# Depthwise 3x3 convolutions: from nine VectorE passes to nine TensorE products with diagonal weights

## The chip, the cores and the metric

The kernel runs on one core of a Trainium2 chip. The metric is the device time of that core in microseconds (us). Engines are named as in the profile: PE (TensorE; PEld its weight loads), DVE (VectorE), ACT (ScalarE), POOL (GpSimd), SP (SyncE, which issues most DMAs).

## The reference, cut to what matters

Eight images of 64 channels and 64x64 pixels, fp32, pass through four blocks. Three places compute a depthwise 3x3 convolution (each channel with its own nine weights, zero padding):

```python
# block 0: attention over all 4096 pixels, then
out = conv3x3_depthwise(att, w2); out = relu(bn2(out))
x = bn3(einsum('bchw,oc->bohw', out, w3)) + x
# block 1: two rounds of window attention and an MLP; block 2: dynamic filters and a 1x9 convolution
# block 3: a selective scan of four directions, sixteen states each
xi, z = split(einsum('bhwc,dc->bhwd', ln(x), in_proj_w) + in_proj_b)
xc = silu(conv3x3_depthwise(xi, conv_w) + conv_b)           # 128 channels
y = ln(sum of the four scans of xc) * silu(z);  x = einsum(y, outproj_w) + x
# block 3, last part: channels in four groups, group i max-pooled by 2**i
s_i = repeat(conv3x3_depthwise(maxpool(part_i, 2**i), mfr_w[i]) + mfr_b[i], 2**i)
out = gelu(einsum('bchw,oc->bohw', concat(s_0..s_3), aggr_w) + aggr_b) * n + x
```

## The kernel before, in words

Two images are worked on at once: their 2 x 64 channels are the 128 partitions, and the 4096 pixels are eight chunks of 512 columns (8 rows of 64). There are four such pairs. `front(p)` is everything of pair p up to the inputs of the scan (`layer0`, `layer1`, `layer2`, `scan_sources`), `scans(p)` is its selective scan, and `back(p)` is what follows.

`begin` runs `front(0)` by itself, with `alone` true. Then `scans(p)` goes through 64 units of 512 pixels with eight steps each, 512 steps a pair, two states a step. In a step, POOL multiplies B by du (L1788), ACT makes the exponentials `dad` (L1810), DVE runs the two recurrences (L1813), POOL and DVE multiply by C (L1824, L1827), and PE sums the states into `yd` (L1839), two or three steps later. Fetches of B and C are DMAs on SP's queue. For the last pair, and during the attention, DVE takes more of the products with C (`own`).

Beside the steps of `scans(p)` a generator hands out `back(p-1)` and `front(p+1)` piece by piece: each `yield` names a cost, and a step takes so many pieces that the costs grow evenly over the steps. For the last pair there is only `back(2)`, at twice the pace; `back(3)` comes with the last units and after them. The program's order is the generator's; a list scheduler then places every instruction by priority and its own estimate of when an engine is free, so an engine's queue may hold pieces ahead of older steps. Each engine works its queue in order.

The convolutions are in `_Direct.dwconv` (L1249): for a chunk, the first tap is a multiplication of the shifted, padded image by the channel's weight (L1257 or L1259) into a PSUM bank, and the other eight are multiply-adds on that bank (L1255), all on DVE.
- In `layer0` the result `cacc` goes through ACT (Relu, batch norm) to the product `pw` (L1348).
- In `scan_sources`, one image at a time, the result is `xacc`: all 128 channels, from the padded `XI`, with the bias in the first tap. ACT applies Silu (`xcv`, L1653), copies it transposed (`XT`), and sends it off by DMA; `z` (L1672) comes from a product of its own, `pz`.
- In `back`, the normalised image `F` is max-pooled three times. Each pooled image is convolved on DVE (`net.dwconv`, L436 and L438) and widened by ACT into `big` (L1909). Then each chunk is convolved (`sacc`), copied by ACT (`S`), and multiplied with its 1x1 weights (L1922); three more products (L1926) add the pooled groups, and Gelu follows (L1933).

PSUM's eight banks are divided: three for chunk results of the front (`f`), one for its accumulators, three for the scan (`da`), one for `yd`.

Of the kernel before, what the change touches and what calls it, by code (L numbers as in the profile page):

```python
# [9 lines left out]
F32 = mybir.dt.float32  # L10
AF = mybir.ActivationFunctionType
ALU = mybir.AluOpType
# [3 lines left out]
B, C, HH, WW = 8, 64, 64, 64  # L16
L = HH * WW
P = 128
CH = 512
# [3 lines left out]
TAPS = 9  # L23
# [1136 lines left out]
class _Direct:  # L1160
# [73 lines left out]
    def normed(self, wk, srcs, cen, avg, eps, out_view=None, bufs=None):  # L1234
# [11 lines left out]
        nc.scalar.activation(sd, sd, AF.Exp, scale=-0.5)  # L1246
        return pc, sd

    def dwconv(self, dst, pad, at, n, wt, bias, cost=0.5):  # L1249

        nc = self.nc
        for t in range(TAPS):
            src = pad[:, at + t // 3 : at + t // 3 + n, t % 3 : t % 3 + 64]
            if t:
                nc.vector.scalar_tensor_tensor(dst, src, wt[:, t : t + 1], dst, ALU.mult, ALU.add)  # L1255
            elif bias is None:
                nc.vector.tensor_scalar(dst, src, wt[:, 0:1], None, ALU.mult)  # L1257
            else:
                nc.vector.tensor_scalar(dst, src, wt[:, 0:1], bias, ALU.mult, ALU.add)  # L1259
            yield cost  # L1260


    def front(self, p):
# [5 lines left out]
    def layer0(self, p):  # L1269


        nc, tc, w, net, half = self.nc, self.tc, self.w, self.net, self.HALF
        X = self.flat("X")
        nc.sync.dma_start(X, self.net.x[2 * p : 2 * p + 2].rearrange("b c h w -> (b c) (h w)"))
        att = self.padded("att")
        VT = self.flat("VT").rearrange("p (t c) -> p t c", c=P)

        def at(rows, t):
            return X[rows, t * P : (t + 1) * P]

        with self.work("w0") as wk:
            for g in range(8):
                pv = self.bank("pval", (P, 4, P))
                nc.tensor.matmul(pv, lhsT=net.ones[0:1, :], rhs=net.b1row.rearrange("o a c -> o (a c)").unsqueeze(1).to_broadcast([1, 4, P]), start=True, stop=False)
                for j in range(4):
                    nc.tensor.matmul(pv[:, j, :], lhsT=at(slice(0, P), 4 * g + j), rhs=net.w1bd, start=False, stop=(j == 3))
                nc.scalar.activation(VT[:, 4 * g : 4 * g + 4, :], pv, AF.Relu)
                yield 3

            parts = wk.tile([P, 2, 32, NCH], F32, name="parts", tag="parts", bufs=1)  # L1290
            self.dense = 1
            for jc in range(NCH):
                po = self.total("po")

                def weigh(t, es):
                    for im in range(2):
                        nc.tensor.matmul(  # L1297
                            po[half[im]], lhsT=VT[:, t, half[im]], rhs=es[im], start=(t == 0), stop=(t == 31)
                        )

                last = None
                for t in range(32):
                    ss = [self.bank(f"s{im}") for im in range(2)]
                    for im in range(2):
# [12 lines left out]
                    last = (t, es)  # L1317
                    yield 3.6
                weigh(*last)
                nc.vector.tensor_copy(self.rows(att, jc), self.img(po))  # L1320

            self.dense = 0
            sums = net.sums[:, p]
            nc.vector.tensor_reduce(sums, parts, AX.X, ALU.add)
            rec = wk.tile([P, 2, 32], F32, name="rec", tag="rec", bufs=1)
            nc.vector.reciprocal(rec, sums)
            for g in range(8):
                pr = self.bank("prec")
                for j in range(4):
                    for im in range(2):  # L1330
                        nc.tensor.matmul(
                            pr[half[im], j * P : (j + 1) * P],
                            lhsT=rec[:, im, 4 * g + j : 4 * g + j + 1].to_broadcast([P, 64]),
                            rhs=w["ident"],
                            start=True,
                            stop=True,
                        )
                d = self.rows(att, g)
                nc.vector.tensor_tensor(d, d, self.img(pr), ALU.mult)
                yield 3  # L1340
        with self.work("w0b") as wk:
            for c in range(NCH):
                acc = self.bank("cacc", (P, 8, 64))
                yield from self.dwconv(acc, att, 8 * c, 8, w["dw2"], None, 0.52)
                cv = wk.tile([P, 8, 64], F32, name="cv", tag="cv")
                nc.scalar.activation(cv, acc, AF.Relu, scale=net.bn23[:, 0:1], bias=net.bn23[:, 1:2])
                pw = self.bank("pw")
                nc.tensor.matmul(pw, lhsT=w["w3bd"], rhs=cv, start=True, stop=True)  # L1348
                nc.scalar.activation(pw, pw, AF.Identity, scale=net.bn23[:, 2:3], bias=net.bn23[:, 3:4])
                x = X[:, c * CH : (c + 1) * CH]  # L1350
                nc.vector.tensor_tensor(x, x, pw, ALU.add)
                yield 2.25
        return X
# [271 lines left out]
    def scan_sources(self, p, X2):  # L1625
# [2 lines left out]
        x2 = self.memory("x2")  # L1628
        with tc.tile_pool(name="w3", bufs=2) as wk:
            H = self.flat("H3")  # L1630
            for c in range(NCH):
                cols = slice(c * CH, (c + 1) * CH)
                nc.sync.dma_start(x2[:, cols], X2[:, cols])
# [4 lines left out]
            for im in range(2):  # L1638
# [9 lines left out]
                XT = self.flat("XT").rearrange("p (w h) -> p h w", h=64)  # L1648
                for c in range(NCH):
                    acc = self.bank("xacc", (P, 8, 64))  # L1650
                    yield from self.dwconv(acc, pad, 8 * c, 8, w["cw"], w["cb"])
                    cv = wk.tile([P, 8, 64], F32, name="xcv", tag="xcv")
                    nc.scalar.activation(cv, acc, AF.Silu)  # L1653
                    last = nc.scalar.activation(XT[:, 8 * c : 8 * c + 8, :], cv, AF.Copy)
                    nc.scalar.dma_start(xc[:, c * CH : (c + 1) * CH], cv.rearrange("p a b -> p (a b)"))
                    yield 1.4
# [5 lines left out]
                for c in range(NCH):  # L1662
# [5 lines left out]
                        start=True,  # L1668
                        stop=True,
                    )  # L1670
                    z = wk.tile([P, CH], F32, name="z", tag="z")
                    last = nc.scalar.activation(z, pz, AF.Silu, bias=w["in_b"][:, 1:2])  # L1672
                    nc.scalar.dma_start(zs[:, c * CH : (c + 1) * CH], z)
                    yield 1.4
# [186 lines left out]
    def back(self, p):  # L1861
# [26 lines left out]
                yield 4.2  # L1888
        with tc.tile_pool(name="w5", bufs=1) as wk:
            prev, n, ups = F, 64, []  # L1890
            for i in range(1, 4):
                n //= 2
                at = (0, 1024, 1536)[i - 1]
# [4 lines left out]
                net.pad_border(pool, n + 2, nc.vector)  # L1898
                h2 = hf.rearrange("p (h two) w -> p h two w", two=2)
                nc.vector.tensor_tensor(pool[:, 1 : n + 1, 1 : n + 1], h2[:, :, 0, :], h2[:, :, 1, :], ALU.max)  # L1900
                if i == 1:
                    cv = big[:, 0:1024].rearrange("p (a b) -> p a b", b=n)
                else:
                    cv = wk.tile([P, n, n], F32, name=f"cv{i}", tag=f"cv{i}")
                net.dwconv(cv, pool, w["mw"][:, i, :], w["mb"][:, i : i + 1], n)
                k = 2**i
                at = (2048, 0, 1024)[i - 1]
                up = big[:, at : at + 64 * n].rearrange("p (a b) -> p a b", b=64)
                nc.scalar.activation(  # L1909
                    up.rearrange("p h (w k) -> p h w k", k=k), cv.unsqueeze(3).to_broadcast([P, n, n, k]), AF.Copy  # L1910
                )
                ups.append(up)
                prev = pool
                yield 7
            for c in range(NCH):
                cols = slice(c * CH, (c + 1) * CH)
                acc = self.bank("sacc", (P, 8, 64))
                yield from self.dwconv(acc, F, 8 * c, 8, w["mw"][:, 0, :], w["mb"][:, 0:1])
                S = wk.tile([P, 8, 64], F32, name="S", tag="S", bufs=2)
                nc.scalar.activation(S, acc, AF.Copy)  # L1920
                pa = self.bank("pa", (P, 8, 64))
                nc.tensor.matmul(pa, lhsT=w["agT"][:, 0, :], rhs=S, start=True, stop=False)  # L1922
                for i in range(1, 4):
                    k = 2**i
                    r = 8 // k
# [4 lines left out]
                        start=False,  # L1930
                        stop=(i == 3),
                    )
                last = nc.scalar.activation(pa, pa, AF.Gelu, bias=w["aggr_b"])  # L1933
                nc.vector.tensor_tensor(pa, pa, self.rows(F, c), ALU.mult)
                nc.vector.tensor_tensor(X[:, cols], X[:, cols], pa.rearrange("p a b -> p (a b)"), ALU.add)
                nc.sync.dma_start(out[:, cols], X[:, cols])
# [53 lines left out]
```

## Time and profile before

| | us |
|---|---|
| median of 3 runs (lowest, highest) | 12034.72 (12024.86, 12036.76) |
| the profiled execution | 12027.92 |
| its span, first to last instruction | 12026.1 |
| busy: PE, DVE, POOL, ACT | 9286.0, 8501.9, 7496.6, 7041.5 |
| mean granted PE clock | 0.856 |
| layer 0's convolution, `cacc`: alone; beside scans | 56; 132, 136, 136 |
| scan_sources from its first H to the last z, beside scans | 232, 219, 224 |
| back from the pooling to the end of the values that follow, pairs 0 and 1 | 181 |
| back of pair 2 from the pooling on, beside the last scans | 514 |

The stages were found by the first and last instruction on a tile. In the rows of stretches, each engine has its busy time and, as (x), its instructions, followed by the granted PE clock (1.0 is full speed), the share of the DMA engines and GB/s. In a group's row, after the bar, stand the busy time, the mean ns of one, and the idle time of the engine just before it, with what ended that. In the page's slices each digit is the busy share of a fortieth of the span, in tenths. One fp32 matrix product appears as two records on PE.

### The profile page before, as it was taken

Reading aid. Unit: us, or ns where it says so; the run is one execution under the profiler, and the core shown is the slowest. Engines: PE = TensorE matmul, PEld = TensorE weight load, DVE = VectorE, ACT = ScalarE, POOL = GpSimd, SP = SyncE. Lnnn points to the kernel's source line nnn. Section 1 sums busy time; section 2 is a strip of 40 time slices with the busy share of each in tenths; the row PEclk is TensorE's granted clock in tenths of the full one; section 3 lists DMA queues with packets and bytes.
Section 4 is the critical chain, followed back from the end, with each engine's and each line's share of the span. In section 5 each row is a group of like instructions: output and inputs, shape, how many; then the busy total and the mean of one; then the engine's idle time right before and its main releaser. Section 6 shows DMA issues by size and latency. Waiting matters only on the chain. (4 is left out here: it accounts for less than half of the span.)

```text
span 12026.1 us, 158030 instructions
## 1 busy us (share of the span) xinstructions
PE 9286.0 (77%) x54038; PEld 2996.5 (25%) x54038; DVE 8501.9 (71%) x10005; ACT 7041.5 (59%) x15950; POOL 7496.6 (62%) x3843
## 2 busy tenths in 40 slices
PE   9977799978878569996788666998787956565556
PEld 2234222224322112222342112222333211111111
DVE  0043567787778784668777776667777778999998
ACT  5545367756665656665665555666666465455554
POOL 0000066677778674667877784567678768878994
PEclk9988889989989689998998778998998967676667
DMA  0000055554445553444444463444344446556663
GB/s 20 1 2 2 34 155 149 149 152 126 133 131 158 166 163 93 144 136 133 136 124 129 149 191 109 124 137 147 118 125 142 134 158 201 172 170 203 206 200 123
DMA packets 779763, 1576.81 MB, mean 131 GB/s; under 512 B 89281, under 2 KB 89409, under 8 KB 778177
## 3 DMA queue, kind: packets, MB, share of 16 engines
q1 hardware_dynamic: 736320, 1443.18, 39.1%
q10 hardware_dynamic: 42624, 123.44, 3.7%
q8 instruction: 427, 7.00, 0.2%
q14 instruction: 392, 3.20, 0.1%
HBM read 1197.16 MB, written 100.66 MB: 108 GB/s over the span
## 5 line engine op out<-in xcount | busy, mean ns | idle before, releaser
L1788 POOL TENSOR_TENSOR vd<-B,du 128x1024 f32<-128x1024 f32 x2048 | 4797.5, 2361 | 2693.1 <-DMA B<-rows 1758.1
L1839 PE MATMUL yd<-vd,pack 128*64 128x512 f32 x8192 | 2807.8, 726 | 863.2 <-POOL vd L1827 486.1
L1810 ACT ACTIVATE dad<-du,As 128x512 f32<-128x512 f32 x4096 | 2726.9, 682 | 798.2 <-DVE vd L1827 377.6
L1813 DVE TENSOR_TENSOR_SCAN hd<-dad,carry,vd 128x512 f32<-128x512 f32 x1989 | 2500.8, 1272 | 418.7 <-ACT dad L1810 369.0
L1827 POOL TENSOR_TENSOR vd<-hd,C 128x512 f32<-128x512 f32 x1293 | 1646.4, 1277 | 1068.7 <-DVE hd L1813 1061.2
L1813 DVE TENSOR_TENSOR_SCAN dad<-dad,carry,vd 128x512 f32<-128x512 f32 x1595 | 2014.9, 1278 | 144.2 <-ACT dad L1810 142.1
L1311 ACT ACTIVATE e<-s 128x512 f32<-128x512 f32 x2048 | 1201.5, 591 | 630.0 <-PE s L1305 628.3
L1824 POOL TENSOR_TENSOR vd<-hd,C 128x1024 f32<-128x1024 f32 x488 | 1150.4, 2357 | 631.1 <-DVE hd L1813 388.8
L1305 PE MATMUL s<-X 64*128 64x512 f32 x4096 | 1452.4, 647 | 85.6 <-ACT e L1311 66.2
L1839 PEld LDWEIGHTS yd<-vd,pack 128*64 128x64 f32 x8192 | 636.5, 157 | 2724.0 <-issue 1204.0
L1827 DVE TENSOR_TENSOR vd<-dad,C 128x512 f32<-128x512 f32 x1827 | 1216.1, 678 | 114.7 <-ACT carry L1821 85.9
L1297 PE MATMUL po<-e,VT 128*64 128x512 f32 x4096 | 1206.7, 626 | 17.1 <-ACT e L1311 13.9
L1821 ACT ACTIVATE carry<-dad 128x1 f32<-128x1 f32 x1597 | 267.5, 169 | 829.7 <-DVE dad L1813 752.8
L1821 ACT ACTIVATE carry<-hd 128x1 f32<-128x1 f32 (+1 forms) x1559 | 309.5, 201 | 723.7 <-DVE hd L1813 710.6
L1305 PEld LDWEIGHTS s<-X 64*128 64x128 f32 x4096 | 399.3, 186 | 1123.1 <-issue 837.2
L1750 PE MATMUL pdd<-xs,xdt 128*128 128x512 f32 x512 | 361.6, 795 | 305.5 <-issue 127.3
L1463 PE MATMUL w_av<-wide,vals 64*32 64x64 f32 x16384 | 496.7, 227 | 124.1 <-DVE w_oc L1492 86.2
L1320 DVE COPY att<-po 128x512 f32<-128x512 f32 x32 | 22.0, 687 | 678.7 <-PE po L1297 678.6
L1463 PEld LDWEIGHTS w_av<-wide,vals 64*32 64x32 f32 x16384 | 410.9, 113 | 272.3 <-issue 157.3
L1474 PE MATMUL w_av<-wide,each 64*32 64x128 f32 x8192 | 467.9, 283 | 3.8 <-issue 3.8
L1451 ACT ACTIVATE wide<-wide 128x512 f32<-128x512 f32 x512 | 311.1, 628 | 261.8 <-DVE wide L1450 261.5
L1243 PE MATMUL pv<-n_sq,pack 128*128 128x512 f32 x576 | 346.7, 686 | 139.7 <-ACT n_sq L1241 127.5
(246 smaller groups left out, 11144.3 us busy)
## 6 DMA issues: line engine op xcount, KB each, us to landing
B<-rows SPq DMA_DIRECT2D x2048, 256.0 KB, 3.5
C<-rows SPq DMA_DIRECT2D x2048, 256.0 KB, 3.5
du<-du SPq DMA_DIRECT2D x384, 512.0 KB, 5.9
du<-du ACTq DMA_DIRECT2D x128, 512.0 KB, 5.0
xs<-xt SPq DMA_DIRECT2D x128, 256.0 KB, 3.9
xs<-xc SPq DMA_DIRECT2D x128, 256.0 KB, 3.9
xc<-xcv ACTq DMA_DIRECT2D x64, 256.0 KB, 2.1
zs<-z ACTq DMA_DIRECT2D x64, 256.0 KB, 3.6
```

Source lines behind the costliest of these rows:

```text
L1297: nc.tensor.matmul(po[half[im]], lhsT=VT[:, t, half[im]], rhs=es[im], start=(t == 0), stop=(t == 31))
L1305: nc.tensor.matmul(ss[im], lhsT=at(half[im], t), rhs=X[half[im], jc * CH : (jc + 1) * CH], start=True, stop=True)
L1311: nc.scalar.activation(e, ss[im], AF.Exp, scale=C**-0.5, accum_out=parts[:, im, t, jc : jc + 1])
L1463: nc.tensor.matmul(self.av[rows, 0, x % 4 + j], lhsT=net.vals[half[im], x + j, 4 * g + h], rhs=es[g][half[im], j, h], tile_position=(64 * ...
L1474: nc.tensor.matmul(self.av[rows, 1, x % 4 : x % 4 + 2], lhsT=net.each[half[im], 32 - HD - HD * h : 64 - HD - HD * h], rhs=es[g][half[im], ...
L1788: self.nc.gpsimd.tensor_tensor(v, self.twice(st["B"]), self.units[i // 8]["du"][:, :, 1], ALU.mult)
L1810: nc.scalar.activation(da, u["du"][:, j, 0], AF.Exp, scale=net.As[:, k, n : n + 1])
L1813: nc.vector.tensor_tensor_scan(along(to), along(da), along(v[:, j]), first, ALU.mult, ALU.add)
L1821: nc.scalar.activation(cs, ends, AF.Copy)
L1824: st["w"] = nc.gpsimd.tensor_tensor(v, h, self.twice(CC), ALU.mult)
L1827: m = engine.tensor_tensor(v[:, j], hs[j], CC, ALU.mult)
L1839: m = nc.tensor.matmul(u["y"][self.HALF[j]], lhsT=w["fold"], rhs=st["v"][:, j], start=(i % 8 == 0), stop=(i % 8 == 7))
```

## The change

`spread_taps` fills a tile of nine 128x128 matrices on ACT: for each tap the identity (or, in the back, the 1x1 weights `agT`) with each row scaled by its channel's weight for that tap. `taps_sum` then computes a chunk's convolution as nine products of PE that add up in one PSUM bank, with the shifted image as the moving operand, and yields after every third with three times the cost. With `n=5`, used in the first front (`alone`), five taps go to PE and four stay on DVE.

In `scan_sources` the bias moves into the Silu, and `xcv` and `z` share a pair of buffers. In `back`, for all pairs but the last, the pooled convolutions go to PE too, ACT widens them with the bias straight from PSUM, and for the full-size one the 1x1 product is folded into the nine matrices: `S` and its product go away, and its bias, multiplied once (`pmb`), joins Gelu's. The last pair's back stays as it was. The `diag` tile has one buffer.

```diff
+    def spread_taps(self, wk, wt, base=None):
+        d = wk.tile([P, TAPS, P], F32, name="diag", tag="diag", bufs=1)
+        for t in range(TAPS):
+            self.nc.scalar.activation(
+                d[:, t], self.w["ident"] if base is None else base, AF.Identity, scale=wt[:, t : t + 1]
+            )
+        return d
...
+    def taps_sum(self, dst, diag, pad, at, cost, stop=True, wt=None, n=TAPS):
+        nc = self.nc
+        for t in range(TAPS):
+            src = pad[:, at + t // 3 : at + t // 3 + 8, t % 3 : t % 3 + 64]
+            if t < n:
+                nc.tensor.matmul(dst, lhsT=diag[:, t], rhs=src, start=(t == 0), stop=stop and t == n - 1)
+            else:
+                nc.vector.scalar_tensor_tensor(dst, src, wt[:, t : t + 1], dst, ALU.mult, ALU.add)
+            if t % 3 == 2:
+                yield cost
...
         with self.work("w0b") as wk:
+            diag = self.spread_taps(wk, w["dw2"])
...
-                yield from self.dwconv(acc, att, 8 * c, 8, w["dw2"], None, 0.52)
+                yield from self.taps_sum(acc, diag, att, 8 * c, 1.56, wt=w["dw2"], n=5 if self.alone else TAPS)
...
             H = self.flat("H3")
+            diag = self.spread_taps(wk, w["cw"])
...
-                    yield from self.dwconv(acc, pad, 8 * c, 8, w["cw"], w["cb"])
-                    cv = wk.tile([P, 8, 64], F32, name="xcv", tag="xcv")
-                    nc.scalar.activation(cv, acc, AF.Silu)
+                    yield from self.taps_sum(acc, diag, pad, 8 * c, 1.5, wt=w["cw"], n=5 if self.alone else TAPS)
+                    cv = wk.tile([P, 8, 64], F32, name="xcv", tag="xz")
+                    nc.scalar.activation(cv, acc, AF.Silu, bias=w["cb"])
...
-                    z = wk.tile([P, CH], F32, name="z", tag="z")
+                    z = wk.tile([P, CH], F32, name="z", tag="xz")
...
+            alone = p == B // 2 - 1
...
+                    diag = self.spread_taps(wk, w["mw"][:, i, :])
+                    m = min(n, 512 // n)
+                    for r in range(0, n, m):
+                        cv = self.bank("cvs", (P, m, n))
+                        for t in range(TAPS):
+                            nc.tensor.matmul(
+                                cv,
+                                lhsT=diag[:, t],
+                                rhs=pool[:, r + t // 3 : r + t // 3 + m, t % 3 : t % 3 + n],
+                                start=(t == 0),
+                                stop=(t == TAPS - 1),
+                            )
+                        nc.scalar.activation(
+                            up[:, r : r + m].rearrange("p h (w k) -> p h w k", k=k),
+                            cv.unsqueeze(3).to_broadcast([P, m, n, k]),
+                            AF.Identity,
+                            bias=w["mb"][:, i : i + 1],
+                        )
...
+            if not alone:
+                near = self.spread_taps(wk, w["mw"][:, 0, :], w["agT"][:, 0, :])
+                pm = self.bank("pmb")
+                nc.tensor.matmul(pm[:, 0:1], lhsT=w["agT"][:, 0, :], rhs=w["mb"][:, 0:1], start=True, stop=True)
+                ab = wk.tile([P, 1], F32, name="ab", tag="ab")
+                nc.vector.tensor_tensor(ab, pm[:, 0:1], w["aggr_b"], ALU.add)
...
+                else:
+                    pa = self.bank("pa", (P, 8, 64))
+                    yield from self.taps_sum(pa, near, F, 8 * c, 1.5, stop=False)
...
-                last = nc.scalar.activation(pa, pa, AF.Gelu, bias=w["aggr_b"])
+                last = nc.scalar.activation(pa, pa, AF.Gelu, bias=ab)
```

More of the change, by code (lines that the diff above doesn't have):

```diff
@@ L1255, in dwconv @@
                 nc.vector.scalar_tensor_tensor(dst, src, wt[:, t : t + 1], dst, ALU.mult, ALU.add)
-            elif bias is None:
-                nc.vector.tensor_scalar(dst, src, wt[:, 0:1], None, ALU.mult)
             else:
@@ L1900, in back @@
                 nc.vector.tensor_tensor(pool[:, 1 : n + 1, 1 : n + 1], h2[:, :, 0, :], h2[:, :, 1, :], ALU.max)
[L1901 to L1905, printed above, removed]
                 k = 2**i
@@ L1908, in back @@
                 up = big[:, at : at + 64 * n].rearrange("p (a b) -> p a b", b=64)
-                nc.scalar.activation(
-                    up.rearrange("p h (w k) -> p h w k", k=k), cv.unsqueeze(3).to_broadcast([P, n, n, k]), AF.Copy
-                )
+                if alone:
+                    if i == 1:
+                        cv = big[:, 0:1024].rearrange("p (a b) -> p a b", b=n)
+                    else:
+                        cv = wk.tile([P, n, n], F32, name=f"cv{i}", tag=f"cv{i}")
+                    net.dwconv(cv, pool, w["mw"][:, i, :], w["mb"][:, i : i + 1], n)
+                    nc.scalar.activation(
+                        up.rearrange("p h (w k) -> p h w k", k=k), cv.unsqueeze(3).to_broadcast([P, n, n, k]), AF.Copy
+                    )
+                else:
+                    diag = self.spread_taps(wk, w["mw"][:, i, :])
[10 more added lines that the diff above has]
+                            )
+                        nc.scalar.activation(
+                            up[:, r : r + m].rearrange("p h (w k) -> p h w k", k=k),
+                            cv.unsqueeze(3).to_broadcast([P, m, n, k]),
+                            AF.Identity,
+                            bias=w["mb"][:, i : i + 1],
+                        )
                 ups.append(up)
@@ L1914, in back @@
                 yield 7
+            ab = w["aggr_b"]
+            if not alone:
[4 more added lines that the diff above has]
+                nc.vector.tensor_tensor(ab, pm[:, 0:1], w["aggr_b"], ALU.add)
             for c in range(NCH):
                 cols = slice(c * CH, (c + 1) * CH)
[L1917 to L1922, printed above, removed]
+                if alone:
+                    acc = self.bank("sacc", (P, 8, 64))
+                    yield from self.dwconv(acc, F, 8 * c, 8, w["mw"][:, 0, :], w["mb"][:, 0:1])
+                    S = wk.tile([P, 8, 64], F32, name="S", tag="S", bufs=2)
+                    nc.scalar.activation(S, acc, AF.Copy)
+                    pa = self.bank("pa", (P, 8, 64))
+                    nc.tensor.matmul(pa, lhsT=w["agT"][:, 0, :], rhs=S, start=True, stop=False)
+                else:
+                    pa = self.bank("pa", (P, 8, 64))
+                    yield from self.taps_sum(pa, near, F, 8 * c, 1.5, stop=False)
                 for i in range(1, 4):
```

## The prediction, made before the changed kernel was run

> **What bounds the kernel now.** I read the page first. No engine is full over the whole span (PE 77%, DVE 71%, POOL 62%), so what counts is each stage. The slices show where:
>
> ```profile
> PE   9977799978878569996788666998787956565556
> ...
> DVE  0043567787778784668777776667777778999998
> ...
> PEclk9988889989989689998998778998998967676667
> ```
>
> In slices 14, 23-24 and from 33 on PE falls to 5 or 6 and its clock mostly to 6 or 7, while DVE holds 7, and from slice 34 on 8 or 9. Next the groups by line, for the operation that is to move:
>
> ```profile
> L1255 DVE SCALAR_TENSOR_TENSOR xacc<-XI,pack,xacc 128x512 f32<-128x512 f32 x512 | 356.1, 751 | 0.4
> ...
> L1255 DVE SCALAR_TENSOR_TENSOR sacc<-F,pack,sacc 128x512 f32<-128x512 f32 x256 | 188.8, 754 | 0.9
> L1255 DVE SCALAR_TENSOR_TENSOR cacc<-att,pack,cacc 128x512 f32<-128x512 f32 x256 | 186.9, 747 | 0.2
> ```
>
> A tap costs DVE 0.75 us (each chunk's first, a TENSOR_SCALAR, 0.74 to 0.81), with almost no idle time before it. Last the stages, found by when each tile is written, here for the second image pair's front, the first pair's back, and the last scans:
>
> ```profile
> core 0: us, PE busy (x) PEld busy (x) DVE busy (x) ACT busy (x) POOL busy (x), PEclk, DMA share, GB/s
> ...
> 2536.00:2668.00 132.00, 62.79 (x136) 14.28 (x134) 130.86 (x158) 63.19 (x134) 117.08 (x58) 0.70 0.48 148
> 2671.00:3423.00 752.00, 620.86 (x8690) 286.55 (x8688) 569.61 (x697) 496.19 (x1002) 572.68 (x281) 0.93 0.45 135
> 3881.00:4113.00 232.00, 115.63 (x201) 27.71 (x200) 179.73 (x233) 155.21 (x230) 121.47 (x60) 0.60 0.50 165
> 4409.00:4433.00 24.00, 0.00 (x0) 0.00 (x0) 23.83 (x29) 1.51 (x3) 9.06 (x4) 0.53 0.34 102
> 4433.00:4590.00 157.00, 99.32 (x246) 40.23 (x248) 131.85 (x187) 80.93 (x132) 66.58 (x36) 0.72 0.36 115
> 4600.00:5430.00 830.00, 800.66 (x2662) 212.08 (x2660) 501.79 (x529) 567.40 (x1651) 481.26 (x259) 0.98 0.42 126
> 10430.00:10944.00 514.00, 297.79 (x602) 64.05 (x600) 479.21 (x544) 284.37 (x583) 395.68 (x210) 0.71 0.55 167
> 10979.00:11690.00 711.00, 419.47 (x930) 91.89 (x932) 681.72 (x728) 367.12 (x906) 672.80 (x365) 0.65 0.68 205
> ```
>
> In order: layer 0's convolution (DVE 99%), the windows (PE 83%), scan_sources (DVE 77%, taps and scan waiting for each other through ACT), back's pooled convolutions (DVE 99%, PE idle), back's full-size one, layer 0's attention (PE 96%), back beside the last scans (DVE 93%), the last scans alone (DVE 96%, POOL 95%). So taps are on the path in every stage that has them.
>
> **The price of a tap on PE.** An fp32 product is two records in the trace. Back to back, full array, 512 columns:
>
> ```profile
> 1243.39 7.09 PE L1617 MATMUL py<-taps,pack 128*128 128x512 f32 x16
> ```
>
> (7.09 - 0.59 for the last one)/15 = 0.433 us a record, 0.867 us a product. At the lower clock, L1664's four records in 3.78 us are 0.85 each, 1.71 us a product. "TensorE: Matmul & The Clock Gate" of the Trainium skill, Back-to-back issue gap, gives N/2.4 + 2.5 ns, 216 ns here: nine taps 1.9 us. By the row they cost 7.8 us, against 6.8 us on DVE. I take the row: PE pays more than DVE saves, and the gain can only come from PE having room.
>
> Over the kernel DVE loses 256 + 512 + 216 full taps (743 us) and 81 pooled ones (68 us); PE gains 984 - 24 full products, 54 pooled ones of 512 columns, 27 of 256 and 27 of 64: 894 us at full clock.
>
> **Which clock.** The same page, Part 1, says the array starts at half clock and gets the full one after about 3.4 us of sustained work. By that rule nine taps warm it themselves. The stage rows say 0.60 and 0.70 today, with PE half idle; the 96% busy attention has 0.98, the windows 0.93. I take 0.93; the other end is a rival below.
>
> **Part by part**, against the profiled execution (span 12026, time 12028 us). The order in which the two built programs hold their instructions (it has no times) says what stands beside the taps.
> - *Front of pair 0, no scans* (56 us for layer 0, 127 for scan_sources). Five taps on PE, four on DVE. Layer 0: 8 x 6 products x 0.867 = 42, plus 3 for the last DVE taps, 3 to fill: 48, so -8. Scan_sources: 112 products (80 taps, 16 pi, 16 pz) are 97/0.93 = 104; with the DVE tail and the step from image to image I take 115: -12. Together **-20** (-5 to -35).
> - *Layer 0's convolution beside scans, three times* (132, 136, 136 us). PE: 80 products (72 taps, 8 pw) 69.4; in the new order 13 scan steps stand among them (24 before), each four yd records in two pairs that overlap, 0.87 us; 3 us of pdd and pbc: 84/0.93 = 90 us. That is -44. But 11 steps now come later, in the windows. There a step costs 1.1 us of PE if PE is the limit, and 752/141 = 5.3 us (the stage's time by its 141 products of B and du on POOL, one a step) if each comes at full price: 13 to 59 us. PE is 83% busy there and nearest, so 23. **-20** each, -60 (-31 to +15 each).
> - *scan_sources, three times* (232, 219, 224 us). PE: 176 products 152.6, 30 steps 26, pdd and pbc 6.5: 185/0.93 = 199. The refill at each image's start (pi, ACT, XI, first taps) costs about 5 us twice: 210. **-15** each, -45 (-40 to +20). Silu now waits for PE instead of DVE; the state exponentials (dad) queue behind it on ACT, and scans behind those, as they do now (ACT waits 101 us for xacc today). Of yd's slack (summed two or three steps late, eight v buffers) a group of 9 to 10 taps, 8 us, takes about a step and a half. The shared xz buffers hold an xcv for some 4 us (Silu 0.6, XT 1.1, its DMA 2.1) out of about 12 a chunk: nothing. No DMA is added; those of xc and zs keep their places on ACT's queue.
> - *Back of pairs 0 and 1* (24 + 157 us). DVE loses its solid pooled block. PE gets 18 products (15.6), 9 of half width (3.9), 9 small (1), with four fills of diag between: the single buffer makes ACT wait for PE's last tap of the level before, the dads behind it; about 35 us with the max pooling. Then 96 products without a yd among them: 83. Gelu 3, values as now 31: 152. Meanwhile ACT stands in seven Gelus in a row and the scan stops; 8 to 9 steps come in the attention, PE-bound, at 1.1 us: 10. 162 for 181; for a slower start I take **-15** each, -30 (-40 to +19).
> - *Back of pair 2 beside the last scans* (514 us, 120 steps, 4.28 a step). 54.5 + 22.7 = 77 us leave a DVE that is 93% busy; alone the scans take 711/209 = 3.40 a step, with POOL at 95%, so POOL is next. PE there is 58% busy. I take three quarters: **-57** (-77 to -20).
> - *Filling diag*: 20 times nine 128x128 ACT operations, at 0.28 us (the same shape in the setup, L325) 50 us of ACT. ACT is 45 to 70% busy in these stages, and its table loads (1.28 us each) fall from 205 to 125 in the new order. Nothing; without that cover +50.
>
> Sum: -20 - 60 - 45 - 30 - 57 = -212, that is 11816; the median of the runs lies 6.8 above the profiled one: **11825 us**.
>
> **The rivals.**
> - *PE at a low clock* (slower). One mechanism: gaps between tap groups, while PE's in-order queue waits for POOL's products (vd) before a yd, keep the clock near today's 0.70 to 0.72 in layer 0's convolution and scan_sources. Their PE work is 84 + 185 = 269 us a pass, and 360 us is spent today; with 33 for displaced steps and refills the point is 269/(360 - 33) = 0.82. At 0.72: 374 + 33 = 407, +47 three times; first front +10; backs -10, last scans -20: +121, **12155 us**. For it: granted 0.60 today, and in one such stage (3889 to 4082 us) yd's rows show 28 us of idle time that ended with vd from POOL. Against: every stage with PE over 80% has 0.93 or more.
> - *Steps displaced at full price.* The scan sets the pace and what is skipped beside taps is paid later: layer 0's convolution +15 three times, backs +19 twice, the rest as above: -39, **11995 us**. For it: POOL is 89% busy in the convolution stage (117 of 132), so steps can't get much quicker there. Against: PE, not POOL, fills the stages where they land.
> - *Everything fills well*: the good ends, 35 + 93 + 120 + 80 + 77 = 405, **11630 us**.
> - That taps stay on DVE is excluded by the order: it holds 1,065 fewer of them.
>
> **How the numbers follow.** Likeliest 0.63 (own range 11700 to 11920), displaced steps 0.18, low clock 0.09, good ends 0.10. The range 11700 to 12000 leaves out most of the good ends and the slow rival. A measurement tells about 0.2%, 24 us. Faster: 0.63 + 0.10 + most of the displaced = 0.86; within 0.2% 0.05; slower 0.09.
>
> **What would show it.** Right: layer 0's convolution shrinks from 132-136 to about 90 us with PE over 85% at a clock over 0.9, and the windows grow by 15 to 30; scan_sources at about 210; each back's first 181 at about 165, the block of 96 products near 83 us with scans stopped; the last scans' back at about 4.28 - 57/120 = 3.8 us a step. Wrong: a clock under 0.82 in the tap stages, PE waiting for vd between groups, or windows and attention growing by what the convolutions lost.

## The result, and the profile after

The changed kernel takes 11,993 to 12,028 us, median 12011.96, against 12031.61 for the kernel before, run beside it: ratio 0.9984, 95% interval 0.9975 to 0.9992. It is faster by some 20 us where 210 were forecast, and outside the range. The profiled execution took 12011.7 us, its span 12009.9, 16.2 less than before.

What was to move did move: DVE's busy time fell from 8501.9 to 7806.3 us, PE's rose from 9286.0 to 9980.9, the mean clock from 0.856 to 0.898. The slices of the changed kernel's page:

```profile
PE   9977999998888779998788978999877986675656
...
DVE  0033367767778474666777555666777748989998
...
PEclk9998989999989889999998989999999987786677
```

PE is now fuller and warm nearly to slice 32. DVE has become lighter in the same slices, and only the end is as it was. So the work changed engines, and the time did not follow. Stretches of the changed kernel, as in the prediction: layer 0's convolution, the windows, scan_sources of two passes, the back's block of 96 products, layer 0's attention, two pieces of scan_sources (see below), and the back beside the last scans:

```profile
core 0: us, PE busy (x) PEld busy (x) DVE busy (x) ACT busy (x) POOL busy (x), PEclk, DMA share, GB/s
2533.00:2629.00 96.00, 91.34 (x219) 32.80 (x216) 42.52 (x45) 32.80 (x70) 61.28 (x30) 0.98 0.35 103
2671.00:3423.00 752.00, 620.08 (x8696) 285.57 (x8696) 588.91 (x714) 495.44 (x1012) 605.34 (x296) 0.92 0.49 142
3890.00:4126.00 236.00, 202.24 (x463) 73.02 (x462) 81.13 (x85) 140.69 (x210) 115.03 (x56) 0.87 0.50 155
4462.00:4546.00 84.00, 83.76 (x195) 36.90 (x196) 29.51 (x36) 23.34 (x39) 6.99 (x5) 1.00 0.25 73
4600.00:5430.00 830.00, 799.53 (x2636) 212.14 (x2633) 517.64 (x547) 568.28 (x1652) 501.76 (x269) 0.98 0.45 130
6778.00:7010.00 232.00, 204.69 (x460) 73.97 (x458) 76.84 (x81) 125.92 (x192) 111.42 (x54) 0.87 0.49 152
10440.00:10700.00 260.00, 214.72 (x560) 68.66 (x562) 230.57 (x265) 169.38 (x355) 215.92 (x116) 0.91 0.60 185
6857.00:6896.00 39.00, 29.94 (x49) 9.57 (x47) 7.56 (x12) 23.79 (x34) 17.27 (x8) 0.64 0.70 222
6971.00:7010.00 39.00, 20.75 (x34) 5.38 (x30) 11.49 (x15) 20.91 (x30) 16.46 (x8) 0.62 0.81 266
```

Layer 0's convolution has gone from 132 to 96 us with PE 95% busy at a clock of 0.98. The block of 96 products takes 84 us at full clock (83 forecast), and the back of pair 2 with the scans behind it is 52 us shorter. But scan_sources, with DVE at a third, is as long as ever: 236 and 232 us.

Cut at the first and last instruction on a tile, the two traces give each term of the prediction (us, profiled executions; a layer's windows are counted up to layer 2's first tap, scan_sources from its first tap to its last `z`; from there the kernel before has 224, 214 and 217 us; the 232, 219 and 224 of the table before run from the last H, not from the first):

| term | forecast | measured |
|---|---|---|
| front of pair 0 alone | -20 | +3: layer 0 -10, scan_sources +11, the rest +2 |
| layer 0's convolution beside scans, and the windows after it | -60 | -36, -37, -37 and +42, +32, +30: -7 |
| scan_sources beside scans | -45 | +11, +17, +15: +44 |
| backs of pairs 0 and 1, and the attention after them | -30 | -20, -19 and +21, +17: 0 |
| back of pair 2 and the last scans | -57 | -52 |
| all else | 0 | -5 |
| sum | -212 | -16 |

Only the back of pair 2 came out as forecast. For scan_sources, PE's queue shows where the time stands (timeline of the changed kernel, second pass, between the pair's two images):

```profile
6836.08 7.99 PE L1275 MATMUL xacc<-XI,diag 128*128 128x512 f32 x18
...
6862.76 3.78 PE L1685 MATMUL pz<-H,pack 64*128 64x512 f32 x4 [4.58 <-ACT xcv L1674]
...
6880.30 1.22 PE L1685 MATMUL pz<-H,pack 64*128 64x512 f32 x1 [2.86 <-ACT z L1693]
...
6883.73 12.31 PE L1664 MATMUL pi<-H,pack 64*128 64x512 f32 x14 [0.78 <-ACT XI L1667]
6895.97 9.18 PE L1275 MATMUL xacc<-XI,diag 128*128 128x512 f32 x18
```

Nine taps are 18 records in 7.99 us, the forecast price, without a gap. Then 41 us pass between the last tap of one image (6855.1) and the first of the next (6896.0). In them PE makes `pz`, waits for ACT, and makes the next image's `pi` at 0.88 us a record, at a granted clock of 0.64; DVE has 7.6 us of work. In the kernel before, `pz` begins while taps still run on DVE, which end at 6846.5, and PE has gaps between its products. The last `pz` and most of `pi` stand in a break there too, until the next image's taps begin at 6874.1:

```profile
6829.52 2.07 PE L1664 MATMUL pz<-H,pack 64*128 64x512 f32 x2 [9.37 <-ACT xcv L1653]
6835.08 2.07 PE L1664 MATMUL pz<-H,pack 64*128 64x512 f32 x2 [3.49 <-ACT z L1672]
...
6859.82 8.90 PE L1643 MATMUL pi<-H,pack 64*128 64x512 f32 x10 [1.10 <-ACT z L1672]
```

The row of that break, at a granted clock of 0.50:

```profile
6846.50:6874.00 27.50, 24.09 (x32) 7.09 (x30) 9.07 (x13) 16.94 (x28) 13.26 (x7) 0.50 0.52 191
```

After the second image another 39 us follow, where the kernel before had 27. So the two runs of taps became shorter, 77 and 75 us instead of 78 and 82, and the two breaks longer by 13 and 12: together the +17 of this pass. The other two passes show the same, with breaks of 37 to 47 us instead of 27 to 31. ACT's timeline in the last break: the transposed copies' DMAs, then a `z` that waited 10.41 us, then table loads, as ACT goes back and forth between Exp and Silu:

```profile
6978.40 7.65 ACTq L1679 DMA_DIRECT2D xt<-XT  x4
...
6988.79 0.69 ACT L1693 ACTIVATE z<-pz,pack 128x512 f32<-128x512 f32 x1 [10.41 <-DMA xt<-XT]
...
7001.79 1.28 ACT L1693 ACT_TABLE_LOAD   x1 [1.69 <-DMA zs<-z]
```

### The profile page after: what moved, and what is told of

It is laid out like the page before. It is cut to its first block, busy times and chain, and to the rows that moved or that the text cites. A ratio compares the mean times of both kernels' runs of the same rounds, so it can differ in the third digit from the quotient of the medians.

```text
span 12009.9 us, 161406 instructions
## 1 busy us (share of the span) xinstructions
PE 9980.9 (83%) x56180; PEld 3350.9 (28%) x56180; DVE 7806.3 (65%) x8943; ACT 6974.8 (58%) x16029; POOL 7487.9 (62%) x3843
## 5 line engine op out<-in xcount | busy, mean ns | idle before, releaser
L1860 PE MATMUL yd<-vd,pack 128*64 128x512 f32 x8192 | 2705.0, 705 | 668.8 <-POOL vd L1848 466.5
L1316 PE MATMUL po<-e,VT 128*64 128x512 f32 x4096 | 1210.3, 627 | 19.3 <-ACT e L1330 16.2
L1316 PEld LDWEIGHTS po<-e,VT 128*64 128x64 f32 x4096 | 235.7, 136 | 850.5 <-issue 570.8
```

What stands on the lines that cost most here:

```text
L1316: nc.tensor.matmul(po[half[im]], lhsT=VT[:, t, half[im]], rhs=es[im], start=(t == 0), stop=(t == 31))
L1860: m = nc.tensor.matmul(u["y"][self.HALF[j]], lhsT=w["fold"], rhs=st["v"][:, j], start=(i % 8 == 0), stop=(i % 8 == 7))
```

## The experiments

The first theory was that the order lost the gain of scan_sources: `z`'s work, once hidden beneath DVE's taps, stands behind PE's. Its rival: PE's own work in that stage is as long as DVE's was, in whatever order. For layer 0 and the backs: the scan steps that no longer run beside them are paid in the next stage. Times are medians, each ratio is to the kernel before on the same chip, and where two runs are compared ("us less", "us more"), it is their distances from the kernel before.

**The parts alone.** *only_l0*, *only_backs01* and *only_last_back* are the kernel before with one part; *no_scan* is the changed kernel with `dwconv`, its Silu and separate buffers put back in scan_sources.

> The kernel before with only layer 0's convolution on TensorE. By the prediction's terms this part alone wins 8 + 60 us: 11965. By the stages of the changed kernel's trace it wins 12 us in the first front and 6 in the three passes, since each of the 11 scan steps that leave the convolution costs 2.4 us in the windows: about 12015.

Measured: 12002.11 us, 0.9979 (0.9971 to 0.9987), 26 us less than before. Nearer to the traces than to the forecast.

> The kernel before with only the backs of pairs 0 and 1 on TensorE. By the stages of the changed kernel's trace each back is 19 us shorter, and the attention behind it, which takes the scan steps that stood beside it, 14 to 17 longer: about 12022. By the prediction's term, 15 us each: about 11998. If the runs of the single parts add up to the run without scan_sources (88 us; layer 0 alone 26, the back of pair 2 alone 50), 12 us are left for these two: about 12017.

Measured: 12016.21 us, 0.9992 (0.9984 to 1.0001), 10 us less. The attentions of the second and third pass had 162 steps instead of 153 in the trace.

> The kernel before, with only the back of pair 2 (the one beside the last scans) on TensorE. If the gain of 53 us that the trace shows there (from the last write of u in the stage before to the end of the back) is this part's own: about 11980. If it was only bought by work that the other parts left or took away: within 20 us of the kernel before, 12032.

Measured: 11981.27 us, 0.9958 (0.9944 to 0.9971), 52 us less: its own gain.

> The changed kernel with scan_sources' convolution put back on VectorE, with its own buffers; everything else stays changed. The stages' traces say that scan_sources on TensorE lost 11, 17 and 15 us in the three passes and about 14 in the first front where 8 to 9 were to be won by layer 0: by them this kernel is 55 to 60 us faster than the changed one, about 11955, and 75 us faster than the one before. If the parts don't add (the scheduler places other scan steps beside the rest): 11990 to 12030.

Measured: 11945.75 us, 0.9928 (0.9915 to 0.9942), 88 us less. The three single parts add up to the same 88. So the parts add, and scan_sources on PE took 68 of them away, with all that came with it.

**Scan_sources: buffers, order, engine.** First the buffers (*split*; to make room, `diag` has a pool of its own, and the norm's tiles are freed before):

```diff
-                    cv = wk.tile([P, 8, 64], F32, name="xcv", tag="xz")
+                    cv = wk.tile([P, 8, 64], F32, name="xcv", tag="xcv")
...
-                    z = wk.tile([P, CH], F32, name="z", tag="xz")
+                    z = wk.tile([P, CH], F32, name="z", tag="z")
```

> The changed kernel, but with two buffers for the convolution's result and two for z in scan_sources again, instead of two for both. If the shared buffers cost time (z's Silu waiting until the transfer of a convolution's result has freed one), scan_sources falls from 232 us to 215 to 222 a pass and the kernel gets 30 to 50 us faster than the changed one (about 11970). If what costs is the order in which TensorE takes the work (all taps of an image first, then its z products, then the next image), the order is the same here and the time stays within 15 us of the changed kernel's 12012. If TensorE's total work is the bound, it stays too.

Measured: 11994.98 us, 0.9970 (0.9959 to 0.9981), 19 us less than the changed kernel, and the two intervals overlap. scan_sources beside scans stayed at 237, 232 and 232 us, so the shared buffers are not what costs there. They cost 11 us in the first front (from its first H to the last z 143.2 us instead of 154.6), where a `z` waited 7.4 us for `xcv`'s transfer in the changed kernel.

Then the order (*zmix*): the loop over `pz` is joined with the loop over chunks.

```diff
                     nc.scalar.dma_start(xc[:, c * CH : (c + 1) * CH], cv.rearrange("p a b -> p (a b)"))
-                    yield 1.4
-                for s in range(4):
-                    nc.scalar.dma_start(
-                        xt[:, 1024 * s : 1024 * s + 1024],
-                        XT.rearrange("p h w -> p w h")[:, 16 * s : 16 * s + 16, :].rearrange("p w h -> p (w h)"),
-                    )
-                for c in range(NCH):
                     pz = self.bank("pz")
...
                     nc.scalar.dma_start(zs[:, c * CH : (c + 1) * CH], z)
-                    yield 1.4
+                    yield 2.8
+                for s in range(4):
+                    nc.scalar.dma_start(
+                        xt[:, 1024 * s : 1024 * s + 1024],
+                        XT.rearrange("p h w -> p w h")[:, 16 * s : 16 * s + 16, :].rearrange("p w h -> p (w h)"),
+                    )
```

> As the kernel with separate buffers, but z's product, its Silu and its transfer for chunk c come right after the convolution of chunk c, instead of after all eight. By the theory of the order (z's work, which lay beneath VectorE's taps before, now stands behind TensorE's taps, and leaves TensorE idle and cold between the images and after the last one): scan_sources falls from 232 us to 185 to 195 a pass, the first front by 15, and the kernel to about 11890, that is 1% below both. By the theory that TensorE's work in this stage is simply as long as VectorE's was: no change in the stage beyond 10 us, 11985 to 12015. If the scan steps that are not done beside it are paid later at full price, the stage shrinks but the last scans or the windows grow, and the kernel stays at 11990 to 12015.

Measured: 12112.59 us, 1.0068 (1.0054 to 1.0081): longer than the kernel before, although scan_sources took 198, 190 and 194 us. The attention of the second pair took 1062 us instead of 938, the first round of windows 339 instead of 283. ACT's timeline at the end of the first front names the cause:

```profile
1520.66 1.28 ACT L442 ACT_TABLE_LOAD   x1
...
1521.95 1.28 ACT L1678 ACT_TABLE_LOAD   x1
...
1523.95 1.28 ACT L1775 ACT_TABLE_LOAD   x1
```

L442 loads the table that has both log and exp, once for all scan steps to come. Here it stands ahead of the last convolution's Silu (L1678), which loads its own; after that every use of Exp and Ln loads a table for itself. The groups of ACT during the attention (1560 to 2640 us), Ln at L1778, Exp at L1833:

```profile
L1778 ACT ACT_TABLE_LOAD x25 | 32.1, 1283 | 0.4
L1833 ACT ACT_TABLE_LOAD x25 | 32.1, 1283 | 0.2
```

The changed kernel has none there. *zmix2* loads the common table behind both Silus (`log_exp` returns its instruction):

```diff
-                    nc.scalar.activation(cv, acc, AF.Silu, bias=w["cb"])
+                    silu = nc.scalar.activation(cv, acc, AF.Silu, bias=w["cb"])
-                net.log_exp(last)
+                net.behind(net.log_exp(last), silu)
```

> The kernel with z's product right after each chunk's convolution, and the common activation table of log and exp loaded behind the last Silu of both kinds (in the run before, the load came ahead of the last convolution's Silu, so that the two functions loaded tables in turn through the whole attention of the second pair: 50 loads and 125 us). scan_sources was 190 to 198 us a pass there, the first front 28 us shorter than in the changed kernel. By the theory of the order both gains now reach the end: about 11895, 1.1% below the kernel before. If TensorE's work is the bound and the shortened stage is only paid in the next one: 11985 to 12015.

Measured: 11891.16 us, 0.9886 (0.9871 to 0.9901), as the theory of the order said. That was not yet a proof: *before_zmix* makes the same reordering in the kernel before, with all taps on DVE.

> The kernel before, taps on VectorE as they were, with only the order of scan_sources changed: z's product, Silu and transfer after each chunk's convolution. By the theory of the order z's products cost nothing before because TensorE stood idle beneath VectorE's taps; what can be won is the tail behind the last tap alone (27 us in two of the three passes, 31 in the third and 15 in the first front): 0 to 25 us a pass, 11950 to 12035. If the reordering is worth its 40 us a pass whichever engine has the taps: about 11890, and then the taps on TensorE win nothing in this stage.

Measured: 11939.36 us, 0.9925 (0.9912 to 0.9939), 87 us less, and scan_sources 186, 186 and 186 us. Its second pass:

```profile
6729.00:6915.00 186.00, 97.78 (x177) 22.33 (x176) 169.63 (x223) 154.55 (x215) 108.26 (x53) 0.61 0.52 171
```

**The theory of the order fell** as the cause: `z` at the end cost the kernel before 28 to 37 us a pass as well. And 186 is less than the 190 to 196 of zmix2. *no_scan_zmix* is zmix2 with `dwconv` put back in scan_sources, so only the engine of these taps differs; *src8* is zmix2 with `n=8` there.

> The kernel with z beside its chunk (11891 us), but scan_sources' taps on VectorE; layer 0 and the backs stay on TensorE. It differs from that kernel in nothing but the engine of these taps. If nine taps on TensorE lose by their own price (scan_sources 186 us a pass with taps on VectorE 91 to 95% busy, 190 to 196 with TensorE 98% busy, in the same order): about 11865, 20 to 35 us below. If the taps only lost by the order, they win here as they were meant to, and this kernel is 20 us or more above 11891.

Measured: 11864.41 us, 0.9858 (0.9842 to 0.9875), 26 us less than zmix2, as the price of PE demands. The two intervals just overlap; the traces agree, with scan_sources 9, 4 and 7 us shorter and the first front's scan_sources equal.

> The kernel with z beside its chunk, and in scan_sources beside scans eight taps of nine on TensorE and one on VectorE. If TensorE's own work sets the length of this stage: 16 products of 0.867 us fewer a pass, the stage 176 to 182 us instead of 190 to 196, and the kernel 25 to 40 us below 11891. If the stage is set by the scans or by ACT: 188 to 196 us and 11885 to 11895; if handing each chunk from TensorE to VectorE costs more than the tap: above 11895.

Measured: 11855.22 us, 0.9857 (0.9839 to 0.9874), 35 us less than zmix2; scan_sources 191, 177 and 180 us, so the first pass gained less than expected. scan_sources of the second and third pass in no_scan_zmix (taps on DVE):

```profile
6714.00:6900.00 186.00, 96.98 (x178) 21.80 (x176) 169.92 (x224) 154.87 (x216) 107.78 (x53) 0.62 0.54 169
9554.00:9740.00 186.00, 97.89 (x178) 22.32 (x176) 169.88 (x224) 154.85 (x215) 108.02 (x53) 0.61 0.53 170
```

In zmix2 (nine taps on PE):

```profile
6718.00:6908.00 190.00, 186.20 (x462) 66.68 (x464) 75.44 (x79) 113.67 (x184) 104.81 (x52) 1.00 0.49 155
9571.00:9765.00 194.00, 190.04 (x465) 67.89 (x464) 75.44 (x79) 114.09 (x185) 105.35 (x52) 0.98 0.49 154
```

DVE at 91% became PE at 98%, at full clock: the bound went to another engine that has as much to do. Two runs put five taps on PE and four on DVE: *zmix2_n5* is zmix2 with `n=5` in layer 0 and scan_sources ("the last" in its expectation is zmix2), *src5* has it in scan_sources alone.

> As the last, and in layer 0 and scan_sources beside scans too only five taps of a chunk on TensorE and four on VectorE (the split that the first front has). If TensorE is the bound of these two stages now (91 of 96 us busy in layer 0's, 190 of 235 before the reordering), both get shorter: layer 0's from 96 to 70 to 80 us, scan_sources from 193 to 170 to 180, about 35 us a pass and 11790 in all. If the chunk's end then waits for VectorE, where four taps queue behind the scans' operations, or the displaced scan steps take the gain: 11880 to 11920.

Measured: 11838.93 us, 0.9841 (0.9827 to 0.9854), between the two expectations: scan_sources came to 169, 164 and 170 us, as in the first, but layer 0's convolution did not get shorter (see below).

> z beside its chunk, five taps of nine on TensorE in scan_sources, but layer 0's convolution beside scans with all nine on TensorE. In the run with five in both, layer 0's convolution was as long as in the kernel before (131 us, 26 to 32 scan steps beside it instead of 12 to 13), and the windows as much shorter; convolution and windows together were within 10 us of each other. If scan steps cost the same in either place, this run is within 12 us of that one: 11830 to 11850. If the placement of the steps matters: 15 us or more away, on either side.

Measured: 11829.15 us, 0.9837 (0.9823 to 0.9850), the lowest of all, though it can't be told from zmix2_n5, as expected if a step costs the same in either place. Its scan_sources of the second and third pass:

```profile
6695.00:6859.00 164.00, 138.10 (x328) 45.61 (x328) 119.39 (x140) 134.28 (x197) 102.68 (x50) 0.91 0.57 179
9522.00:9692.00 170.00, 143.30 (x328) 46.69 (x328) 119.79 (x140) 135.01 (x198) 103.30 (x51) 0.88 0.55 174
```

PE 84%, ACT 80%, DVE 72%: no engine is full, and the stage is 23 to 27 us shorter than in zmix2.

**Layer 0: what the displaced steps cost.** In zmix2_n5 the scheduler kept 26 to 32 steps beside layer 0's convolution (28 to 29 in the kernel before, 12 to 16 in the changed one and in src5). Its rows for that convolution:

```profile
5381.00:5512.00 131.00, 93.05 (x226) 31.95 (x226) 109.56 (x121) 63.98 (x132) 112.56 (x56) 0.85 0.54 160
8215.00:8346.00 131.00, 92.42 (x226) 31.81 (x226) 110.38 (x122) 64.81 (x134) 113.18 (x56) 0.85 0.54 161
```

Forty taps (30 us) have left DVE, and yet it takes 131 us for 26 steps, 5.0 each; before, it was 136 for 28, 4.9 each. The expected 70 to 80 us were wrong: they left out that the steps would come back. Convolution and windows together take 965, 948 and 942 us in zmix2_n5 and 978, 939 and 939 in src5. The three passes add up to 2855 and 2856 us: where the steps stand made no difference here.

*src5_no_l0* is src5 with `dwconv` put back in layer 0.

> As the last, with layer 0's convolution back on VectorE everywhere, the first front too. By the single part's run, layer 0 on TensorE is worth 26 us (12 of them in the first front, where no scan runs): about 11865. If the parts don't add: at or below 11845.

Measured: 11860.63 us, 0.9859 (0.9844 to 0.9874), 31 us above src5: layer 0's part is worth its 26 here too.

*l0cost* is no_scan with a higher price of the taps for the planner, so that more steps stay beside them:

```diff
-                yield from self.taps_sum(acc, diag, att, 8 * c, 1.56, wt=w["dw2"], n=5 if self.alone else TAPS)
+                yield from self.taps_sum(acc, diag, att, 8 * c, 3.4, wt=w["dw2"], n=5 if self.alone else TAPS)
```

> The changed kernel with scan_sources on VectorE (11946 us), and layer 0's convolution declared to the planner at the price that gives it 20 scan steps beside it instead of 13 (24 stood there in the kernel before). If the steps that layer 0's convolution gave up are paid at more in the windows and the attention (2.4 us each by the stages) than they would cost beside the convolution (1.1 us of TensorE): the convolution takes 103 to 110 us instead of 96, the windows' first part 15 to 17 less, and the kernel is at about 11922. If a step costs the same in either place: 11940 to 11952.

Measured: 11973.58 us, 0.9955 (0.9941 to 0.9969), 33 us more than no_scan: neither expectation. Steps beside the convolution rose to 20 to 22 and it took 102 to 113 us, but the higher total also moved 8 more steps to the end (from the last `u` ahead of the back of pair 2 to the end, POOL has 401 products of B and du instead of 393), and that stretch grew by 41 us in a trace that lies 21 us above the run's median. The windows of the second and third pass even grew, by 19 and 11 us, with two steps fewer. Why is open; the run decides nothing about the price of a step.

## Why the prediction was wrong, step by step

- **The price of a tap on PE** was right: (7.99 - 0.59)/17 = 0.435 us a record. Taking the row was right too: the 216 ns of the page cited there are for an isolated product, where an fp32 one of 512 columns took 0.87 us here. **The clock**, taken at 0.93, came to 0.97 to 1.00 wherever nine taps a chunk fill PE; scan_sources as a whole, with its breaks, has 0.87. The rival of the low clock, and with it the slower side, is refuted. The trace agrees with the rule of the Trainium skill cited there (sustained work brings the full clock): the block of 96 products has 1.00, and in the broken work between the images the clock fell to 0.64.
- **Scan_sources failed first, and by most** (forecast -45 and -12, measured +44 and +11). The sum of PE's work, 185 at full clock, was right: zmix2 shows 186 to 192. What failed is the step "the refill at each image's start (pi, ACT, XI, first taps) costs about 5 us twice: 210". In this order the break between the images takes 41 us and the one after the second image, which the sum left out, 39. And the 210 was set against 232, 219 and 224 us of which I took DVE for the cause, at 77% busy, though 28 and 27 us of them were such breaks already. With `z` moved, the same DVE taps need 186. So the order, not DVE, made that stage long, and the change keeps the order. In the better order nine taps cost 7.8 us on PE and 6.8 on DVE, and PE's sum for the stage is 190 where DVE's stage takes 186.

  By the runs, the 68 us that this part took are about 20 for the shared buffers (forecast "nothing"; split), 25 for the engine (zmix2 against no_scan_zmix; their traces show about 20 in scan_sources beside scans), and the remaining 25 for an order that hurts PE's taps more than DVE's: the reordering is worth 98 us with the taps on PE (split against zmix2) and 75 with them on DVE (no_scan against no_scan_zmix). The intervals leave each of the three uncertain by about 20 us, and the last is only what is left.
- **Layer 0's convolution** (forecast -60, measured -7 in the traces, and -26 with the first front in its own run). The step that failed is "11 steps now come later". In the trace 13 to 16 left the convolution: 28 to 29 stood there, not 24 (POOL's x58 and x30 in the rows are about two a step), since I had counted them by the built order, among PE's instructions; the windows took 15 to 16 more and grew by 30 to 42 us, 1.9 to 2.8 a step, where 2.1 was taken. The gain of 44 was 36 to 37. So the price was about right and the number of steps too low. This is the rival "steps displaced at full price" in part: its 15 us a pass of loss did not come, a gain of 2 did.
- **Backs of pairs 0 and 1** (forecast -30, measured 0 in the traces, -10 in the run, which can't be told from none). The back itself was right, 165 for 184 us from the last `u` to the end of the values. The step that failed is "8 to 9 steps come in the attention, PE-bound, at 1.1 us: 10": the attention took 9 steps, but at 1.9 to 2.4 us each. PE is 96% busy there in both kernels, and what a step costs beyond its `yd` is not shown.
- **The back of pair 2** was right in size: -57 forecast, -52 in the trace and in the run. From the last `u` before it to the end, DVE lost 75 us of work and the time fell by 52, so "three quarters" was nearly right. Where the steps stand was not: 57 of them, not 120, are beside the back (227 us from its first pooled image to its last value instead of 519, 4.0 a step), and the others come later.
- **Filling diag** at 0.28 us an operation is 0.39 in the trace; its 180 keep ACT busy for 58 us. "Nothing" was nearly right: what PE waited for it stands behind the bars of its groups, 3.1, 3.4 and 6.9 us. (The terms add up to 11,823 us, not 11,825.)

```profile
L1275 PE MATMUL cacc<-att,diag 128*128 128x512 f32 x512 | 234.2, 605 | 3.1 <-ACT diag L1253 3.1
L1275 PE MATMUL pa<-F,diag 128*128 128x512 f32 x432 | 197.5, 604 | 3.4 <-ACT diag L1253 3.4
...
L1941 PE MATMUL cvs<-pool,diag 128*128 128x512 f32 (+2 forms) x216 | 77.8, 510 | 26.4 <-DVE pool L423 19.3 <-ACT diag L1253 6.9
...
L1253 ACT ACTIVATE diag<-pack,pack 128x128 f32<-128x128 f32 x117 | 37.3, 388 | 14.2 <-DVE taps L1619 14.2
```

## What to carry to other kernels

Before work is moved off a busy engine, ask whether the stage is long because that engine is full or because of the order of its work: here the reordering alone won 87 us, and the whole change 20. Then set the new engine's whole sum for the stage, with all that used to hide beneath the old one, against the shortest time that the old one could have had; where both came out alike, here, sharing won (five taps of nine) and moving did not. Work that a shorter stage gives up must be counted in the trace and priced by what the next stage takes for a unit of it.

## What the runs showed of the hardware

The order of two Silus against one table load was worth 216 us (zmix against zmix2): the 50 loads in the attention are 64 us of ACT, but the attention grew by 125; the other 92 came in the convolution and the windows behind it, where loads come in turn too (110 instead of 32). The attention's waits in zmix, then in the changed kernel (engine and operation <- what it waited for: us, times, longest):

```profile
PE s L1324 <- ACT e L1330: 72.2, 36, 2.6
```

```profile
PE s L1324 <- ACT e L1330: 23.0, 21, 2.0
```

And the rows of the two stretches, zmix first, each from the first to the last product `s`:

```profile
1558.00:2620.30 1062.30, 980.40 (x2935) 250.60 (x2936) 670.99 (x702) 725.78 (x1939) 658.62 (x353) 0.87 0.46 132
```

```profile
1577.00:2515.00 938.00, 899.27 (x2937) 243.12 (x2938) 667.83 (x703) 658.96 (x1892) 656.05 (x353) 0.98 0.51 150
```

PE waited 49 us longer for the softmax, in pauses none of which is over 2.6 us. With them the granted clock of the stretch fell from 0.98 to 0.87, and PE was busy 980 us instead of 899 with the same number of records. So of the 125 us, 81 passed with PE busy at the lower clock: more than the pauses themselves. The Trainium skill ("ScalarE: Activation LUTs", Table sets: the hidden batching unit) says that log and exp together need one load of their common set instead of one each; the trace shows that this holds only as long as nothing from another set comes after it.
